# Second layer of a fused convolution kernel: the skip term by ACT, end terms on all rows, a narrower output projection, a new order

## The chip, the cores and the metric

One core of one Trainium2 chip. The time is device microseconds of one execution. The engines are named PE (matmul), DVE, ACT, POOL (elementwise) and SP (which issues the DMAs); each runs its instructions in its own program order and waits on semaphores for the others.

## What is computed

Two layers run one after the other on `x` of 8 x 128 x 128 x 128 (batch, channels, rows, columns), all in float32. The first, a dilated convolution with spectral attention, isn't touched. The second, cut to what matters:

```python
y = conv2d(x, conv_w, padding=1) + conv_b             # 128 -> 128 channels, 3 x 3
seq = y.reshape(B * H * W, 8, 16)                     # the channels of a position: 8 tokens of 16
xi, z = split(seq @ in_proj_w.T)                      # 32 + 32
xc = silu(conv1d(xi))                                 # 4 taps along the tokens
dt, Bm, Cm = split(xc @ x_proj_w.T)                   # 1 + 16 + 16
dt = softplus(dt * dt_proj_w + dt_proj_b)
h = exp(dt * A) * h + dt * Bm * xc                    # a state of 32 x 16, token after token
ym = (sum(h * Cm) + D * xc) * silu(z)
out = ym @ out_proj_w.T                               # back to 128 channels
return x + silu(group_norm(out))
```

## The kernel before

The second layer, `layer1`, works on 256 blocks of 4 image rows (512 positions, `N`). A block's channels are on the 128 partitions, as 4 tokens x 32 inner channels for half of the 8 tokens (`hf` 0 or 1). The state of a position has 32 x 16 entries for each token. It is spread over the partitions as 16 states x 8 channels, with the 32 channels in four groups of 8 (`NG`). A step `s` from 0 to 15 is one token `t = s // 2` and two of the four groups, so a tile has 128 x 2 x 512 elements. The steps that the prediction names:

- `spread_a s` (L824, PE) writes dt times A into a PSUM pair, `exps s` (L835, ACT) takes its exponential in place, `decay s` (L855; L853 for the last token) multiplies it by the state of the token before, in place, and `add s` (L860) adds the new input: both on DVE. The pair is free after add (for s of 14 and 15 after decay).
- `spread_u s` (L824, PE) writes the inputs dt * xc into a PSUM pair, and `inject s` (L847, DVE) multiplies them by B; the pair is free after inject. For s in 4, 5 and 10 POOL does it from a copy laid out by DMA (L845).
- `weigh s` (L866, POOL) multiplies the state by C, and `collect t` (L922, PE) sums the states into `yps`.
- Terms that need no recurrence are taken apart: at the first and the last token the product of a token's own B and C is summed over the states by `ends_sum` (L896, PE, from L888 on POOL), multiplied by the inputs in `own_terms` (L902, DVE), and added to `yps` by `own_add` (L906, PE). The skip term D * xc is written into `yps` by `skip` (L915, PE), which opens the sum of each half.
- `gated hf` (L929, DVE) reads `yps` and multiplies by silu(z); `project_out` (L937, PE), `result` (L947, ACT) and `keep` (L960, SP) end a block. The group norm of an image follows when its last block is out (`norm`), and then `last_load`, `last_act` (L1012), `last_sum` (L1018) and `last_store` finish one block's rows in each pass.

A spread has two matmuls of 32 rows each: for even `s` they use rows 0 to 63 of the array, for odd `s` rows 64 to 127.

PSUM is full: three pairs of banks (slots 0, 1 and 2, the last argument of a spread and of `project_x` and `project_z`), one bank `pm` for all else, and one for `yps`. So a spread waits for the release of what was in its slot before.

No scheduler is at work. The program order of every engine is the written-out list `ORDER`; one pass goes through the list, and each entry says which step it issues, for which block (relative to the pass), and with which arguments:

```python
for i in range(-4, nb + 3):
    for f, ahead, *k in ORDER:
        if live(i + ahead):
            f(i + ahead, *k)
```

So `(exps, 0, 9)` is step 9 of the pass's own block and `(conv, 3, 0)` the first tap of the convolution of the block three ahead. In the text "add 10" is the step with `s` of 10, "a13" and "u2" stand for spread_a 13 and spread_u 2, and a half is written behind the name (skip 0, gated 1).

Of the kernel before, what the change touches and what calls it, by code (L numbers as in the profile page):

```python
# [9 lines left out]
F32 = mybir.dt.float32  # L10
# [6 lines left out]
P = 128  # L17
# [22 lines left out]
def _fields(widths):  # L40
# [13 lines left out]
    ("half", NH * L), ("group", P), ("ends", 4 * NH * DI), ("place", P),  # L54
# [13 lines left out]
def _constants():  # L68
# [42 lines left out]
    put(c1, C1, "place", (k[:, None] == i[None, :] // LP) & (i % LP == np.where(i < DI, 0, LP - 1)[:, None]))  # L111
# [479 lines left out]
def layer1(ctx, tc, x1, w1, c1, out):  # L591
# [34 lines left out]
    place = cf("place")  # L626
# [6 lines left out]
    m_o = const.tile([P, NH, L, G], F32, name="m_o")  # L633
# [8 lines left out]
    with tc.tile_pool(name="l1_prep", bufs=2) as prep:  # L642
# [18 lines left out]
        for hf in range(NH):  # L661
            for l in range(L):
                k = hf * L + l
                nc.vector.tensor_scalar(m_o[:, hf, l, :], wf("out_w"), cf("half")[:, k:k + 1], None, ALU.mult)
# [27 lines left out]
    LAST = (2, 6)  # L692
# [185 lines left out]
    def lay_own(i):  # L878
        d = st8[i]
        d["us"] = wk1.tile([NH * DI, N], F32, name="us")  # L880
        for e, l in enumerate((0, LP - 1)):
            u = d["u", e].rearrange("(d l) n -> l d n", l=LP)
            nc.sync.dma_start(d["us"][e * DI:(e + 1) * DI, :], u[l])
# [6 lines left out]
    def ends_sum(i):  # L890

        d = st8[i]
        d["pm"] = misc()
        for q in range(4):
            for e in range(NH):
                nc.tensor.matmul(  # L896
                    d["pm"][e * DI:(e + 1) * DI, q, :], ends[:, q, e, :], d["cb"], start=True, stop=True)

    def own_terms(i):
        d = st8[i]  # L900
        d["own"] = wk2.tile([NH * DI, N], F32, name="own")
        nc.vector.tensor_mul(d["own"], flat(d["pm"])[0:NH * DI], d["us"])  # L902

    def own_add(i, e):
        d = st8[i]
        nc.tensor.matmul(  # L906
            d["yps"], place[e * DI:(e + 1) * DI, :], d["own"][e * DI:(e + 1) * DI, :], start=False, stop=False,
            skip_group_check=True)

    def skip(i, hf):  # L910
        d = st8[i]
        d["yps"] = p_y.tile([P, N], F32, name="yps")
        for g in range(NG):
            a = slice(g * DI, (g + 1) * DI)
            nc.tensor.matmul(  # L915
                d["yps"][a], m_d[:, a], d["xc"][:, hf, :], start=True, stop=False, skip_group_check=True)
# [14 lines left out]
    def project_out(i, k):  # L931
        d = st8[i]
        if k == 0:
            d["pm"] = misc()
        for n in range(k * RB, (k + 1) * RB):
            j, hf = n // NH, n % NH
            nc.tensor.matmul(  # L937
                d["pm"][:, j, :], d["ym", hf][:, j * C:(j + 1) * C], m_of[:, hf, :],
                start=(hf == 0), stop=(hf == NH - 1))
# [58 lines left out]
    loaded, active = [], []  # L998
# [16 lines left out]
    def last_sum(i):  # L1015
        if active:
            b, r, v, res = active[0]
            nc.gpsimd.tensor_add(res, res, v)  # L1018

    def last_store(i):  # L1020
        if active:
            b, r, v, res = active.pop(0)
            nc.sync.dma_start(out[b, :, r:r + RB, :], res)  # L1023
# [3 lines left out]
        (load, 4), (skip, -1, 1), (add, 0, 3), (keep, -2), (spread_u, 0, 8, 1), (exps, 0, 4), (inject, 0, 9),  # L1027
        (decay, 0, 4), (inject, 0, 8), (end_products, 0), (spread_a, 0, 5, 2), (inject, 0, 5), (turned, 2),
        (exps, 0, 5), (lay_own, 0), (add, 0, 4), (decay, 0, 5), (collect, -1, 4), (collect, -1, 7),
        (last_act, -1), (collect, -1, 5), (spread_a, 0, 6, 0), (spread_u, 0, 11, 1), (project_dt, 1, 0),  # L1030
        (lay_states, 0, 1, 1), (add, 0, 5), (spread_u, 0, 13, 2), (weigh, 0, 2), (inject, 0, 11), (exps, 0, 6),
        (spread_a, 0, 7, 1), (softplus, 1, 0), (last_sum, -1), (lay_inputs, 0, 5), (own_add, -1, 1),
        (decay, 0, 6), (collect, -1, 6), (ends_sum, 0), (inject, 0, 13), (add, 0, 6), (exps, 0, 7),
        (weigh, 0, 3), (weigh, 0, 4), (own_terms, 0), (spread_a, 0, 8, 0), (weigh, 0, 5), (gated, -1, 1),
        (exps, 0, 8), (spread_a, 0, 9, 2), (decay, 0, 7), (project_bc, 1, 0), (skip, 0, 0), (states, 1, 0),
        (decay, 0, 8), (weigh, 0, 6), (add, 0, 7), (collect, 0, 1), (add, 0, 8), (exps, 0, 9), (decay, 0, 9),
        (project_bc, 1, 1), (spread_of, -2), (states, 1, 1), (spread_u, 0, 12, 1), (weigh, 0, 7),
        (inputs, 1, 0), (lay_states, 1, 0, 0), (inject, 0, 10), (own_add, 0, 0), (spread_a, 0, 11, 0),
        (add, 0, 9), (inject, 0, 12), (store_inputs, 1, 2), (project_dt, 1, 1), (lay_inputs, 1, 2),
        (exps, 0, 11), (decay, 0, 11), (collect, 0, 3), (collect, 0, 2), (spread_a, 0, 10, 2),  # L1040
        (softplus, 1, 1), (spread_u, 1, 1, 1), (exps, 0, 10), (add, 0, 11), (project_out, -1, 0),
        (project_out, -1, 1), (inject, 1, 1), (spread_a, 0, 13, 0), (spread_u, 1, 2, 1), (weigh, 0, 9),
        (result, -1), (lay_ends, 1), (exps, 0, 13), (decay, 0, 10), (inputs, 1, 1), (conv, 3, 0), (add, 0, 10),
        (inject, 1, 2), (decay, 0, 13), (spread_a, 0, 12, 2), (exps, 0, 12), (add, 0, 13), (decay, 0, 12),
        (conv, 3, 1), (project_x, 2, 1), (silu_x, 2), (last_store, -1), (weigh, 0, 10), (project_z, 2, 0),
        (conv, 3, 2), (weigh, 0, 8), (add, 0, 12), (silu_z, 2), (spread_u, 1, 0, 1), (gated, 0, 0),
        (weigh, 0, 15), (weigh, 0, 14), (spread_a, 0, 15, 2), (inject, 1, 0), (conv, 3, 3),
        (spread_a, 1, 2, 1), (spread_u, 1, 3, 0), (lay_states, 1, 1, 0), (exps, 0, 15), (weigh, 0, 12),
        (lay_states, 1, 0, 1), (decay, 0, 15), (weigh, 0, 11), (conv, 3, 4), (inject, 1, 3),
        (store_inputs, 1, 5), (spread_u, 1, 7, 2), (spread_a, 0, 14, 0), (exps, 1, 2), (conv, 3, 5),  # L1050
        (decay, 1, 2), (conv, 3, 6), (last_load, 1), (inject, 1, 7), (spread_u, 1, 6, 2), (add, 1, 2),
        (weigh, 0, 13), (spread_a, 1, 3, 1), (exps, 0, 14), (conv, 3, 7), (exps, 1, 3), (decay, 0, 14),
        (inject, 1, 6), (decay, 1, 3), (conv, 3, 8), (inject, 1, 4), (spread_u, 1, 9, 2), (biased, 3),
        (spread_a, 1, 4, 0), (norm, -3), (turn, 3),
# [23 lines left out]
    with tc.manual_schedule(engines={E.PE, E.Activation, E.DVE, E.Pool, E.SP}):  # L1078
        for i in range(-4, nb + 3):
            for f, ahead, *k in ORDER:  # L1080
                if live(i + ahead):
                    f(i + ahead, *k)
        i = nb
        while tails or loaded or active:
            last_load(i)
            last_act(i)
            last_sum(i)
            last_store(i)
# [90 lines left out]
```

## Time and profile before

| | |
|---|---|
| time, median of 3 runs | 13987.08 us (13984.85 to 13987.69) |
| the profiled execution | 13980.7 us; span of the trace 13978.8 us |
| granted TensorE clock | 0.991 |
| PE, DVE, ACT, POOL busy | 97%, 88%, 65%, 89% of the span |
| layer 0 | up to about 2050 us |
| layer 1 | 256 blocks, xc (L748) first at 2049.8 us and last at 13777.6 us |

A line of a group in the profile names the source line, the engine, the operation, the tiles written and read with their shapes, and the count; then busy time, mean duration in ns, and the idle time ahead of it with what ended it. A row of a timeline has the start in us, the duration, the same names, and in brackets the idle time before it with its releaser. A matmul in float32 is two instructions in the trace, each with a weight load (PEld).

### The profile page before, as it was taken

To read this page: it belongs to the slowest core of one execution; us is meant where nothing else is said; L and a number is where in the kernel's file an instruction comes from. 1 tells how busy PE (TensorE), PEld (TensorE's weight loads), DVE (VectorE), ACT (ScalarE), POOL (GpSimd) and SP (SyncE) were. 2 spreads that over 40 slices of the span, in tenths; PEclk is the share of its full clock that TensorE was granted. 3 is DMA by queue.
4 is the path that set the end of the run, shared out by engine and by line. 5 is a ranking of instruction groups with operands and counts; after the bars stand their busy time and mean duration, and the time that the engine had idled before them with its cause. 6 is when DMAs were issued, how large, how long until landed. Compare 5 with 4: busy or idle time off the path is not lost. (4 is left out here: it accounts for less than half of the span.)

```text
span 13978.8 us, 215719 instructions
## 1 busy us (share of the span) xinstructions
PE 13516.8 (97%) x77864; PEld 5468.2 (39%) x77864; DVE 12280.7 (88%) x11971; ACT 9099.3 (65%) x10678; POOL 12431.6 (89%) x6788
## 2 busy tenths in 40 slices
PE   9999999999999999999999999999999999999996
PEld 5676673333333333333333333333333333333332
DVE  3343349999999999999999999999999999999997
ACT  3353356666677777777777777776777777777775
POOL 6656649999999999999999999999999999999996
PEclk9999999999999999999999999999999999999998
DMA  4444446666666666666666666666666666767666
GB/s 134 151 124 123 143 121 133 137 139 134 140 153 156 153 151 154 151 158 152 151 152 153 157 149 157 152 153 153 152 157 151 152 154 153 156 147 157 153 153 178
DMA packets 1199723, 2077.87 MB, mean 149 GB/s; under 512 B 141376, under 2 KB 337984, under 8 KB 1190464
## 3 DMA queue, kind: packets, MB, share of 16 engines
q1 hardware_dynamic: 1198080, 2061.54, 64.0%
q8 instruction: 616, 10.09, 0.3%
q14 instruction: 451, 3.69, 0.1%
q10 hardware_dynamic: 576, 2.55, 0.0%
HBM read 822.01 MB, written 234.88 MB: 76 GB/s over the span
## 5 line engine op out<-in xcount | busy, mean ns | idle before, releaser
L866 POOL TENSOR_TENSOR hc<-h,cc 128x1024 f32<-128x1024 f32 x3584 | 8377.5, 2371 | 655.7 <-PE yps L922 281.3
L835 ACT ACTIVATE s<-s 128x1024 f32<-128x1024 f32 x3584 | 3615.5, 1009 | 2956.7 <-PE s L824 2942.4
L824 PE MATMUL s<-dt,m_a 32*128 32x512 f32 x14336 | 3764.4, 641 | 255.8 <-DVE h L860 189.4
L860 DVE TENSOR_TENSOR h<-s,h 128x1024 f32<-128x1024 f32 x3072 | 3724.5, 1219 | 98.4 <-POOL hc L866 0.9
L855 DVE TENSOR_TENSOR s<-s,h 128x1024 f32<-128x1024 f32 x3072 | 3743.6, 1224 | 8.9 <-ACT s L835 6.6
L847 DVE TENSOR_TENSOR h<-s,bb 128x1024 f32<-128x1024 f32 x2816 | 3420.9, 1215 | 191.0 <-PE s L824 170.1
L824 PE MATMUL s<-u,l_ct 32*128 32x512 f32 x11264 | 3184.0, 641 | 9.0 <-DVE h L860 3.7
L135 PE MATMUL pm<-xin,l_wt 128*128 128x508 f32 (+1 forms) x4608 | 2436.5, 629 | 5.7 <-DVE wk L645 5.0
L845 POOL TENSOR_TENSOR h<-ud,bb 128x1024 f32<-128x1024 f32 x768 | 1825.7, 2377 | 13.3 <-DMA ud<-uw 9.5
L922 PE MATMUL yps<-hc,l_ct 128*32 128x512 f32 x14336 | 1747.4, 598 | 0.9 <-POOL hc L866 0.9
L824 PEld LDWEIGHTS s<-dt,m_a 32*128 32x128 f32 x14336 | 1001.4, 183 | 1470.7 <-DVE h L847 687.4
L824 PEld LDWEIGHTS s<-u,l_ct 32*128 32x128 f32 x11264 | 852.3, 183 | 1420.5 <-issue 809.1
L135 PEld LDWEIGHTS pm<-xin,l_wt 128*128 128x128 f32 x4608 | 729.8, 188 | 1603.4 <-issue 1408.8
L835 ACT ACT_TABLE_LOAD x992 | 1272.7, 1283 | 22.7 <-PE s L824 3.6
L922 PEld LDWEIGHTS yps<-hc,l_ct 128*32 128x32 f32 x14336 | 387.7, 109 | 1200.4 <-issue 984.2
L775 POOL TENSOR_TENSOR u<-dt,xc 128x512 f32<-128x512 f32 x512 | 653.3, 1276 | 50.4 <-ACT dt L770 50.4
L770 ACT ACT_TABLE_LOAD x511 | 655.6, 1283 | 28.7 <-PE pm L765 0.7
L853 DVE TENSOR_TENSOR hc<-s,hc 128x1024 f32<-128x1024 f32 x512 | 623.2, 1217 | 36.1 <-ACT s L835 9.8
L765 PE MATMUL pm<-xc,m_dt 128*128 128x512 f32 x1024 | 577.2, 646 | 1.4 <-ACT yT L737 0.7
L937 PEld LDWEIGHTS pm<-m_o,ym 128*128 128x128 f32 x4096 | 476.5, 191 | 194.8 <-ACT dt L770 192.7
L915 PE MATMUL yps<-xc,m_d 128*32 128x512 f32 x4096 | 548.0, 607 | 0.1
L906 PE MATMUL yps<-own,l_ct 32*128 32x512 f32 x1024 | 547.3, 614 | 0.0
(193 smaller groups left out, 14097.9 us busy)
## 6 DMA issues: line engine op xcount, KB each, us to landing
bb<-all_b SPq DMA_DIRECT2D x1792, 256.0 KB, 5.7
cc<-all_c SPq DMA_DIRECT2D x1792, 256.0 KB, 5.7
ud<-uw SPq DMA_DIRECT2D x1536, 256.0 KB, 4.5
xin<-x SPq DMA_DIRECT2D x152, 768.0 KB, 5.1
xin<-x SPq DMA_DIRECT2D x112, 640.0 KB, 7.1
gn<-xr SPq DMA_DIRECT2D x256, 256.0 KB, 4.2
v<-gn SPq DMA_DIRECT2D x224, 256.0 KB, 4.0
res<-x SPq DMA_DIRECT2D x224, 256.0 KB, 3.3
```

What stands on the lines that cost most here:

```text
L135: nc.tensor.matmul(out[:, a:b, wa:wb], wt[:, t, :], src[:, r + dy + a - base:r + dy + b - base, wa + dx:wb + dx], start=(n == 0), stop=(n ...
L770: nc.scalar.activation(d["dt", hf], flat(d["pm"]), AF.Softplus, bias=wf("dt_b"))
L775: nc.gpsimd.tensor_mul(d["u", hf], d["dt", hf], d["xc"][:, hf, :])
L824: nc.tensor.matmul(d[name, s][:, q], m[a:a + DI, t % LP, :], d[src, t // LP][a:a + DI, :], start=True, stop=True)
L835: nc.scalar.activation(da, da, AF.Exp)
L845: nc.gpsimd.tensor_mul(h, d["ud", t][:, k:k + GP, :], state_row(i, "bb", t))
L847: nc.vector.tensor_mul(h, d["ups", s], state_row(i, "bb", t))
L853: nc.vector.tensor_mul(d["hc", s], da, d["hc", s])
L855: nc.vector.tensor_mul(da, da, d["h", s - GP])
L860: nc.vector.tensor_add(h, d["da", s], h)
L866: nc.gpsimd.tensor_mul(hc, d["h", s if t < L - 1 else s - GP], state_row(i, "cc", t))
L922: nc.tensor.matmul(d["yps"][g * DI:(g + 1) * DI], gather[:, t % LP, :], d["hc", GP * t + g // GP][:, g % GP], start=False, stop=t in LAST, ...
```

## The change

Four things in `layer1`:

- `skip` is an ACT instruction that writes D * xc into `yps`, and the matmuls of the half add to it. Only the first half of block 0 is still opened by PE.
- The end terms are held in 128 rows of 256 columns, not 64 rows of 512: `lay_own` lays the inputs out with four DMAs, `ends_sum` writes four groups of 32 partitions, and `own_add` adds with eight matmuls of 128 rows, 32 outputs and 256 columns, not with one of 32 rows, 128 outputs and 512 columns.
- `project_out` gives each half its own 64 output columns (4 tokens x 16), where before both halves were added up in 128.
- `ORDER` is new. `last_sum` hands over to a list of its own, which `last_store` reads.

```diff
-    put(c1, C1, "place", (k[:, None] == i[None, :] // LP) & (i % LP == np.where(i < DI, 0, LP - 1)[:, None]))
+    put(c1, C1, "place", np.stack([
+        (i // DI == h)[:, None] & (k[:, None] == i[None, :] // LP) & (i % LP == (0, LP - 1)[h % NH])[None, :]
+        for h in range(2 * NH)], 1))
...
-    m_o = const.tile([P, NH, L, G], F32, name="m_o")
+    m_o = const.tile([P, NH, LP, G], F32, name="m_o")
...
-            for l in range(L):
-                k = hf * L + l
-                nc.vector.tensor_scalar(m_o[:, hf, l, :], wf("out_w"), cf("half")[:, k:k + 1], None, ALU.mult)
+            for l in range(LP):
+                nc.vector.tensor_scalar(m_o[:, hf, l, :], wf("out_w"), same4[:, l:l + 1], None, ALU.mult)
...
-    LAST = (2, 6)
+    LAST = (3, 6)
...
-        d["us"] = wk1.tile([NH * DI, N], F32, name="us")
+        d["us"] = wk1.tile([P, N // 2], F32, name="us")
         for e, l in enumerate((0, LP - 1)):
             u = d["u", e].rearrange("(d l) n -> l d n", l=LP)
-            nc.sync.dma_start(d["us"][e * DI:(e + 1) * DI, :], u[l])
+            for h in range(2):
+                a = (h * NH + e) * DI
+                nc.sync.dma_start(d["us"][a:a + DI, :], u[l][:, h * (N // 2):(h + 1) * (N // 2)])
...
         for q in range(4):
             for e in range(NH):
+                a = (q // 2 * NH + e) * DI
                 nc.tensor.matmul(
-                    d["pm"][e * DI:(e + 1) * DI, q, :], ends[:, q, e, :], d["cb"], start=True, stop=True)
+                    d["pm"][a:a + DI, q % 2, :], ends[:, q, e, :], d["cb"], start=True, stop=True)
...
-        d["own"] = wk2.tile([NH * DI, N], F32, name="own")
-        nc.vector.tensor_mul(d["own"], flat(d["pm"])[0:NH * DI], d["us"])
+        d["own"] = wk2.tile([P, N // 2], F32, name="own")
+        nc.vector.tensor_mul(d["own"], flat(d["pm"])[:, 0:N // 2], d["us"])
...
     def own_add(i, e):
         d = st8[i]
-        nc.tensor.matmul(
-            d["yps"], place[e * DI:(e + 1) * DI, :], d["own"][e * DI:(e + 1) * DI, :], start=False, stop=False,
-            skip_group_check=True)
+        for h in range(2):
+            for g in range(NG):
+                a = slice(g * DI, (g + 1) * DI)
+                nc.tensor.matmul(
+                    d["yps"][a, h * (N // 2):(h + 1) * (N // 2)], place[:, h * NH + e, a], d["own"],
+                    start=False, stop=False, skip_group_check=True)

     def skip(i, hf):
         d = st8[i]
         d["yps"] = p_y.tile([P, N], F32, name="yps")
-        for g in range(NG):
-            a = slice(g * DI, (g + 1) * DI)
-            nc.tensor.matmul(
-                d["yps"][a], m_d[:, a], d["xc"][:, hf, :], start=True, stop=False, skip_group_check=True)
+        if i == 0 and hf == 0:
+            nc.tensor.matmul(d["yps"], m_d, d["xc"][:, hf, :], start=True, stop=False, skip_group_check=True)
+        else:
+            nc.scalar.mul(d["yps"], d["xc"][:, hf, :], wf("D"))
...
             nc.tensor.matmul(
-                d["pm"][:, j, :], d["ym", hf][:, j * C:(j + 1) * C], m_of[:, hf, :],
-                start=(hf == 0), stop=(hf == NH - 1))
+                d["pm"][:, j, hf * (W // 2):(hf + 1) * (W // 2)], d["ym", hf][:, j * C:(j + 1) * C], m_of[:, hf, :],
+                start=True, stop=True)
...
-        for i in range(-4, nb + 3):
+        for i in range(-4, nb + 2):
```

The new list, in full:

```python
ORDER = (
    (load, 4), (lay_inputs, 0, 5), (spread_u, 0, 11, 1), (spread_a, 0, 6, 0), (decay, 0, 5),
    (softplus, 1, 0), (inject, 0, 11), (add, 0, 5), (exps, 0, 6), (weigh, 0, 3), (collect, -1, 5),
    (weigh, 0, 5), (ends_sum, 0), (own_terms, 0), (spread_a, 0, 7, 1), (weigh, 0, 4), (decay, 0, 6),
    (exps, 0, 7), (spread_a, 0, 8, 2), (decay, 0, 7), (project_bc, 1, 0), (add, 0, 6), (collect, -1, 6),
    (add, 0, 7), (own_add, -1, 1), (exps, 0, 8), (states, 1, 0), (gated, -1, 1), (project_bc, 1, 1),
    (states, 1, 1), (spread_u, 0, 13, 0), (decay, 0, 8), (inject, 0, 13), (skip, 0, 0), (add, 0, 8),
    (spread_a, 0, 9, 1), (exps, 0, 9), (project_dt, 1, 1), (inputs, 1, 0), (own_add, 0, 0),
    (collect, 0, 1), (decay, 0, 9), (softplus, 1, 1), (weigh, 0, 6), (spread_a, 0, 11, 0),
    (spread_u, 0, 12, 2), (weigh, 0, 7), (project_out, -1, 0), (project_out, -1, 1), (add, 0, 9),
    (lay_states, 1, 0, 0), (inject, 0, 12), (exps, 0, 11), (spread_u, 1, 1, 1), (spread_a, 0, 10, 2),
    (result, -1), (collect, 0, 2), (collect, 0, 3), (decay, 0, 11), (inputs, 1, 1), (conv, 3, 0),
    (inject, 0, 10), (inject, 1, 1), (lay_ends, 1), (exps, 0, 10), (weigh, 0, 9), (add, 0, 11),
    (decay, 0, 10), (weigh, 0, 8), (store_inputs, 1, 5), (spread_u, 1, 2, 1), (add, 0, 10), (inject, 1, 2),
    (spread_a, 0, 13, 0), (exps, 0, 13), (conv, 3, 1), (spread_a, 0, 12, 2), (decay, 0, 13), (add, 0, 13),
    (weigh, 0, 11), (exps, 0, 12), (last_load, 0), (project_x, 2, 1), (lay_states, 1, 1, 0), (silu_x, 2),
    (weigh, 0, 10), (conv, 3, 2), (decay, 0, 12), (project_z, 2, 0), (last_act, 0), (spread_u, 1, 0, 1),
    (silu_z, 2), (store_inputs, 1, 2), (add, 0, 12), (spread_a, 0, 15, 2), (spread_u, 1, 3, 0),
    (inject, 1, 0), (spread_a, 1, 2, 1), (conv, 3, 3), (last_store, -1), (exps, 0, 15), (conv, 3, 4),
    (weigh, 0, 15), (gated, 0, 0), (inject, 1, 3), (spread_a, 0, 14, 0), (decay, 0, 15), (exps, 1, 2),
    (decay, 1, 2), (spread_u, 1, 7, 2), (weigh, 0, 14), (exps, 0, 14), (conv, 3, 5), (add, 1, 2),
    (inject, 1, 7), (conv, 3, 6), (spread_u, 1, 6, 2), (decay, 0, 14), (spread_a, 1, 3, 1), (exps, 1, 3),
    (conv, 3, 7), (weigh, 0, 13), (inject, 1, 6), (decay, 1, 3), (skip, 0, 1), (conv, 3, 8),
    (spread_a, 1, 4, 0), (weigh, 0, 12), (lay_inputs, 1, 2), (biased, 3), (spread_u, 1, 9, 2),
    (lay_states, 1, 0, 1), (exps, 1, 4), (collect, 0, 4), (norm, -2), (turn, 3), (spread_of, -1),
    (add, 1, 3), (spread_u, 1, 8, 1), (turned, 3), (keep, -1), (inject, 1, 9), (spread_a, 1, 5, 2),
    (decay, 1, 4), (project_dt, 2, 0), (inject, 1, 8), (end_products, 1), (inject, 1, 4), (collect, 0, 7),
    (inject, 1, 5), (weigh, 1, 2), (last_sum, 0), (exps, 1, 5), (lay_own, 1), (lay_states, 1, 1, 1),
    (add, 1, 4),
)
```

More of the change, by code (lines that the diff above doesn't have):

```diff
@@ L53 @@
     ("ident", P), ("spread", LP * P), ("gather", LP * DI), ("taps", KC * L), ("same4", LP),
-    ("half", NH * L), ("group", P), ("ends", 4 * NH * DI), ("place", P),
+    ("half", NH * L), ("group", P), ("ends", 4 * NH * DI), ("place", 2 * NH * P),
 ])
@@ L625, in layer1 @@
     ends = cf("ends").rearrange("p (q e d) -> p q e d", e=NH, d=DI)
-    place = cf("place")
+    place = cf("place").rearrange("p (h c) -> p h c", c=P)
     m_u = cf("spread").rearrange("p (l c) -> p l c", c=P)
@@ L996, in norm @@
             norm_of(b)
-    loaded, active = [], []
+    loaded, active, summed = [], [], []
     def last_load(i):
@@ L1016, in last_sum @@
         if active:
-            b, r, v, res = active[0]
+            b, r, v, res = active.pop(0)
             nc.gpsimd.tensor_add(res, res, v)
+            summed.append((b, r, res))
     def last_store(i):
-        if active:
-            b, r, v, res = active.pop(0)
+        if summed:
+            b, r, res = summed.pop(0)
             nc.sync.dma_start(out[b, :, r:r + RB, :], res)
     ORDER = (
-        (load, 4), (skip, -1, 1), (add, 0, 3), (keep, -2), (spread_u, 0, 8, 1), (exps, 0, 4), (inject, 0, 9),
@@ L1028, in layer1 @@
[L1028 to L1052, printed above, removed]
@@ L1053, in layer1 @@
-        (inject, 1, 6), (decay, 1, 3), (conv, 3, 8), (inject, 1, 4), (spread_u, 1, 9, 2), (biased, 3),
-        (spread_a, 1, 4, 0), (norm, -3), (turn, 3),
+        (load, 4), (lay_inputs, 0, 5), (spread_u, 0, 11, 1), (spread_a, 0, 6, 0), (decay, 0, 5),
+        (softplus, 1, 0), (inject, 0, 11), (add, 0, 5), (exps, 0, 6), (weigh, 0, 3), (collect, -1, 5),
+        (weigh, 0, 5), (ends_sum, 0), (own_terms, 0), (spread_a, 0, 7, 1), (weigh, 0, 4), (decay, 0, 6),
+        (exps, 0, 7), (spread_a, 0, 8, 2), (decay, 0, 7), (project_bc, 1, 0), (add, 0, 6), (collect, -1, 6),
@@ L1083, in layer1 @@
         i = nb
-        while tails or loaded or active:
+        while tails or loaded or active or summed:
             last_load(i)
```

## The prediction

> **What bounds the kernel now.** I read the page's shares first, then stretches of 1500 us, then the timelines of single engines.
>
> ```profile
> PE 13516.8 (97%) x77864; PEld 5468.2 (39%) x77864; DVE 12280.7 (88%) x11971; ACT 9099.3 (65%) x10678; POOL 12431.6 (89%) x6788
> ...
> DVE  3343349999999999999999999999999999999997
> ```
>
> The first line has the shares, the second the busy tenths by slice. DVE's low first six slices are layer 0 (to about 2050 us), which the change doesn't touch. In a stretch of layer 1 alone:
>
> ```profile
> 4900.00:6400.00 1500.00, 1464.81 (x8438) 519.11 (x8434) 1460.98 (x1318) 1064.74 (x1179) 1422.89 (x684) 1.00 0.68 152
> ```
>
> PE, DVE and POOL (first, third and fifth figure after the length) are all busy 95 to 98% of the time; ACT 71%. Three queues are nearly full, so no engine's own saving counts by itself. A layer-1 block recurs every 45.85 us (L915's second group at 7022.56 and 7068.41; over all 256 blocks L748's first and last start give 45.99, with the group norms). What closes that period is seen in the timelines of DVE and then PE:
>
> ```profile
> 7048.22 1.23 DVE L860 TENSOR_TENSOR h<-s,h 128x1024 f32<-128x1024 f32 x1
> 7049.36 1.21 DVE L847 TENSOR_TENSOR h<-s,bb 128x1024 f32<-128x1024 f32 x1
> ...
> 7055.28 0.68 DVE L929 TENSOR_TENSOR ym<-yps,zs 128x512 f32<-128x512 f32 x1
> 7056.61 1.22 DVE L847 TENSOR_TENSOR h<-s,bb 128x1024 f32<-128x1024 f32 x1 [0.65 <-PE s L824]
> ```
>
> ```profile
> 7049.50 1.13 PE L824 MATMUL s<-dt,m_a 32*128 32x512 f32 x4 [0.29 <-DVE h L860]
> 7050.55 1.12 PE L135 MATMUL pm<-xin,l_wt 128*128 128x508 f32 x2
> 7051.51 1.88 PE L743 MATMUL s<-yT,m_x 128*128 128x512 f32 x4
> 7053.32 1.13 PE L755 MATMUL s<-yT,m_z 64*128 64x512 f32 x4
> 7054.38 1.12 PE L135 MATMUL pm<-xin,l_wt 128*128 128x512 f32 x2
> 7055.43 0.70 PE L824 MATMUL s<-u,l_ct 32*128 32x512 f32 x2
> ```
>
> PE waits for DVE's add 10 to release a PSUM pair, runs six groups (7.1 us to 7056.61), and DVE waits for the last of them (spread_u 0) in inject 0. So the loop is: DVE from inject 0 (7010.76) to the end of add 10 (7049.46), 38.7 us, and PE from there to inject 0, 7.15 us: 45.85, the whole period. DVE's 38.7 is 38.12 of pure queue (31 starts of 1.13, the last 1.24, two short ones of 0.60, five of 0.13 more where an add directly follows its decay) and 0.58 of small waits. Pure queue per block: DVE 37 x 1.13 + 3 x 0.60 + 7 x 0.13 = 44.5; POOL 17 x 2.32 (seven L866 in 16.26 us) + 2 x 1.24 + 0.42 + 7/8 x 1.24 = 43.5; PE, adding start to start without its waits, 43.7.
>
> **What the Trainium skill says.** "TensorE: Matmul & The Clock Gate", Part 3: matmuls on different 32-row groups run together. The trace agrees, and it matters for what the change takes away:
>
> ```profile
> 7030.82 0.70 PE L824 MATMUL s<-dt,m_a 32*128 32x512 f32 x2
> 7030.83 0.69 PE L906 MATMUL yps<-own,l_ct 32*128 32x512 f32 x1
> ```
>
> The own-term matmul (row group 1) starts 0.01 us after a spread in rows 64 to 127; both are over at 7031.89. Same page, LDWEIGHTS (loading the stationary operand): a load costs its columns / 1.2 ns, 107 for 128. L937's 16 loads fill 1.86 us, 116 each, so that group is load-bound. "PSUM — Partial Sum Buffer", The four PSUM rules: ACT writes leave the has_written bits, and a matmul that doesn't open a group adds where they are set. No run here shows it; it is why block 0's first skip stays on PE. "ScalarE: Activation LUTs", What ACT_TABLE_LOAD costs: 1283 ns; the trace has 1283.
>
> **The change part by part**, per block.
>
> *Skip on ACT.* PE loses 16 instructions: 0.86 to 1.0 us a half, -1.9. ACT gains two 128x512 scaled copies, not in this trace: between L947 (598 ns, no pointer) and L1012 (814, two pointers); I take L956's 0.72 (one), so +1.4. They stand behind gated (DVE) and ahead of the own and collect matmuls, so two waits are new. skip 0 waits in ACT's queue for gated 1, with exps 9, softplus 1 and exps 11 behind it: with the queues laid end to end it starts 8.95 us and ends 9.7 us after decay 5, spread_a 9 ends at 10.4, exps 9 at 11.5, and decay 9 comes at 12.3, so 0.8 us is spare. own_add 0 waits for skip 0 on PE, with collect 1 behind, but PE gets there at 11. Both cost nothing while DVE's queue covers them.
>
> *Table loads.* With last_act between the two silus, loads fall from 992 + 221 for exp and L1012 to 774 + 0: 439 x 1.283 = 563 us less ACT. ACT isn't the bound; nothing, covered by DVE's queue. If L1012's transfer were late it would now hold silu_z and all exps behind it; by the queues it is issued some 9 us ahead, and page part 6 has v landing in 4.0.
>
> *Own terms in 128 rows.* DVE's L902 goes from 512 to 256 columns: 673 to about 425 ns (L440, 260 columns), -0.25 us. PE: ends_sum's 16 instructions spread over four column groups, not two: 1.04 to between 0.5 and 1.0, I take 0.6. own_add had been nearly free; now each is 16 instructions on all rows, which nothing in row groups can accompany. By L922's rate (8 of 512 columns in 0.88) 0.9; by L937's 124 ns each 2.0. I take 0.9, +1.7 over the two. lay_own issues four DMAs for two, about 1.2 us more on SP, which waits for all_b 9 us a block (2319.8 us in 256).
>
> *Output projection of 64 columns.* Half the streaming, but the same 16 loads of 128 columns: 1.98 to 1.85, floor 1.0 if loads were to overlap.
>
> *The order.* Spreads in different row groups pair: before, 10 pairs and 5 single slots; after, 11 pairs and 3, so -1.05 on PE. PE's sum becomes 43.7 - 1.9 + 1.7 - 0.45 - 0.15 - 1.05 = 41.9. DVE has six adjacent decay-add pairs for seven: 44.5 - 0.25 - 0.13 = 44.1. POOL stays at 43.5. last_load starts one block earlier after each norm and runs to the last block, so two, not four, output slices are left for the serial drain, where they come every 5.7 us (13902.23, 13907.91): -11 us once. The other SP steps move within slack (SP issues some 31 us of 45): lay_states 1 waits for POOL's inject 10, lay_inputs 2 for its own store, each several us ahead of its reader.
>
> Now the loop. add 10 no longer leads to spread_u 0 over a slot. In the new order slot 2 goes inject 12, spread_a 10, and PE runs from there without a wait that I find: spread_a 10 with u1 1.07, two collects 1.86, conv 1.05, a13 with u2 1.08, conv 1.05, a12 1.05, project_x 1.81, conv 0.95, project_z 1.06, u0 1.08, and 0.10 to DVE: 12.16 us. DVE from inject 0 to the end of inject 12: 26 x 1.13 + 1.21 + 2 x 0.60 + 0.36 + 3 x 0.13 = 32.5. Sum 44.7, where before it is 38.12 + 7.15 = 45.3. Small waits: before 0.58, of which 0.2 stood at decay 15 and goes; the rest scaled to the shorter stretch 0.32. New: inject 6 stands two places after inject 7, whose slot its spread needs: 1.25 + 1.13 against 2.26, 0.15. Period 45.2, against 45.85: -0.68 us x 256 = -174, and -11: -185. The profiled execution took 13980.7 us (span 13978.8), 0.05% under the median 13987.1; from the median, 13800.
>
> **Rivals.**
>
> *A, the loop above*, chance 0.55: 13800, own range 13720 to 13890 (0.3 us a block either way, for the small waits).
>
> *B, DVE's queue alone.* If the PE stretch is shorter than I count and small waits go, the period is 44.1 plus 0.2 to 0.6: 1.55 to 1.15 less, 13580 to 13680. For it: DVE's sum. Against it: inject 0 stood behind PE 256 times (170.1 us), and the PE stretch is now longer. 0.20.
>
> *C, half of it.* The new order puts two or three waits of 0.2 us elsewhere (inject 3 and exps 15 are within 0.2 to 0.3 of DVE): 13890 to 13958. 0.10.
>
> *D, slower: own_add pays by instruction.* The other loop is add 4, spread_a 6, then all of PE to u0 (27.4: the 41.9 less 14.5 for the groups after u0), then DVE from inject 0 to add 4, 16.85: 44.25, with small waits 44.95. It holds both own_adds, ends_sum and project_out. Each us per own_add counts twice, so at 1.35 each it equals 45.85 and the gain is gone; at L937's 124 ns it is 47.1, +1.3 x 256: up to 14310. For it: 32 new instructions per block, each with a weight load. Against: 32-column loads are cheap (L783: eight in 0.16 us). 0.11.
>
> *E, nothing measurable*, A and D offsetting or the ACT write not taking PE's work away in effect: 0.04. The instruction order shows L915 gone but for one group, so that the change doesn't do what it says is unlikely.
>
> **The numbers.** This kernel's runs tell about 0.2% (28 us) from no change. Faster: A, B and C, 0.85; same 0.04; slower 0.11. The range holds A, B down to 13610, and C: 13610 to 13965; D and the rest of B are left out.
>
> **What would show it.** Right: L929 to inject 0 still has a wait for PE, and PE's start of spread_a 10 follows inject 12; own_add near 0.9 a group; ends_sum near 0.6; L937's group still 1.8; no idle time of DVE behind ACT. Wrong: DVE without a wait at inject 0 (B), own_add groups above 1.35 (D), exps or decay 9 waiting behind skip (C or worse), POOL with less than 1 us of idle time per block.

## The result, and the profile after

The changed kernel takes 13861.68 us (median; 13859.87 to 13864.33), beside 13987.0 on the same chip before: a ratio of 0.9911, interval 0.9894 to 0.9928. That is 125 us less, where 185 were forecast. The profiled execution took 13860.26 us, span 13858.5.

The page's busy line and DVE's slices, which answer to the first two lines shown of before:

```profile
PE 13496.6 (97%) x80938; PEld 5526.0 (40%) x80938; DVE 12211.5 (88%) x11963; ACT 8814.3 (64%) x10753; POOL 12421.6 (90%) x6788
...
DVE  3343349999999999999999999999999999999997
```

PE has 3074 matmuls more and is busy 20 us less; the picture is the old one. The same 1500 us of layer 1 (after the length: PE, PEld, DVE, ACT, POOL):

```profile
4900.00:6400.00 1500.00, 1475.19 (x8888) 530.71 (x8882) 1465.38 (x1330) 1020.60 (x1186) 1434.81 (x691) 1.00 0.69 155
```

By this count all three full queues are a little fuller. PE went from 1464.81 to 1475.19: its instructions were to get 1.8 us a block shorter, and yet it seems nearer to the bound than before. The timelines show why. DVE's rows, with the add 5 of two blocks (L861 at 7023.27 and 7068.59) and inject 0 (7049.27):

```profile
7023.27 1.22 DVE L861 TENSOR_TENSOR h<-s,h 128x1024 f32<-128x1024 f32 x1
...
7049.27 1.23 DVE L848 TENSOR_TENSOR h<-s,bb 128x1024 f32<-128x1024 f32 x1 [0.28 <-PE s L825]
...
7068.59 1.21 DVE L861 TENSOR_TENSOR h<-s,h 128x1024 f32<-128x1024 f32 x1
```

PE's rows of the same block, without those between 7033.03 and 7047.04, none of which has a wait:

```profile
7023.66 2.01 PE L825 MATMUL s<-dt,m_a 32*128 32x512 f32 x8
7025.60 1.06 PE L784 MATMUL pm<-xc,m_bc 128*32 128x512 f32 x8
7026.48 1.04 PE L931 MATMUL yps<-hc,l_ct 128*32 128x512 f32 x8
7027.34 1.05 PE L913 MATMUL yps<-own,l_ct 128*32 128x256 f32 x16
7028.20 1.04 PE L784 MATMUL pm<-xc,m_bc 128*32 128x512 f32 x8
7029.18 1.13 PE L825 MATMUL s<-u,l_ct 32*128 32x512 f32 x4
7030.14 1.02 PE L825 MATMUL s<-dt,m_a 32*128 32x512 f32 x4
7031.09 1.13 PE L766 MATMUL pm<-xc,m_dt 128*128 128x512 f32 x2
7032.15 1.07 PE L913 MATMUL yps<-own,l_ct 128*32 128x256 f32 x16
7033.03 1.04 PE L931 MATMUL yps<-hc,l_ct 128*32 128x512 f32 x8
...
7047.04 1.13 PE L756 MATMUL s<-yT,m_z 64*128 64x512 f32 x4
7048.10 1.13 PE L825 MATMUL s<-u,l_ct 32*128 32x512 f32 x4
```

The first row is a7 and a8 in one; it lasts 2.01 us because a8 stands in it until add 5 has ended at 7024.49 and left slot 2. From a8 (7024.53) PE runs without a pause to u0 (7048.10), and inject 0 waits for u0. So the loop is: PE from a8 to the start of inject 0, 24.74 us, DVE from there to the end of the next add 5 (7069.80), 20.53. Sum 45.27; the period is 45.31 (L825's u0 at 7002.79 and 7048.10), before 45.85. It is not the loop of the forecast, which runs over inject 12 and a10.

A busy PE is in part a waiting one. Two spreads that were to run side by side start one after the other where the second waits for its slot, and the first counts as busy meanwhile. Here are u0, a15, u3 and a2:

```profile
7002.79 1.13 PE L825 MATMUL s<-u,l_ct 32*128 32x512 f32 x4
7003.73 1.13 PE L825 MATMUL s<-dt,m_a 32*128 32x512 f32 x4
7004.69 1.02 PE L825 MATMUL s<-u,l_ct 32*128 32x512 f32 x4
7005.24 1.13 PE L825 MATMUL s<-dt,m_a 32*128 32x512 f32 x4
```

a15 begins when add 12 has ended on DVE (7003.67), a2 when inject 0 has (7005.19). The next group starts at 7006.30, so the four take 3.51 us, where two pairs take 2.1: 1.4 us of waiting. In the same block a5 costs 0.35 us in this way, a6 0.28 and a8 0.88, and PE stands idle for 0.50 ahead of u6. Without them the 45.31 us become 41.9, and that is the PE sum of the forecast. So PE's instructions did get shorter; the time went into waits, most of which the busy share does not show.

Of the pieces, in the same 1500 us (busy time and mean ns of one, then idle time ahead), two of before and then four of after:

```profile
L906 PE MATMUL yps<-own,l_ct 32*128 32x512 f32 x132 | 70.5, 613 | 0.0
L937 PE MATMUL pm<-m_o,ym 128*128 128x128 f32 x528 | 67.7, 281 | 0.0
...
L913 PE MATMUL yps<-own,l_ct 128*32 128x256 f32 x1056 | 69.9, 382 | 0.0
L946 PE MATMUL pm<-m_o,ym 128*128 128x64 f32 x528 | 66.0, 278 | 0.0
L924 ACT ACTIVATE yps<-xc,l_wt 128x512 f32<-128x512 f32 x66 | 45.5, 689 | 3.3
L906 DVE TENSOR_TENSOR own<-pm,us 128x256 f32<-128x256 f32 x33 | 13.7, 414 | 0.0
```

The own term matmuls on PE (L913) come to as much as the old L906 had (70.5 us), L946 to hardly less than L937 (67.7). By starts, an own_add takes 0.86 to 0.88 us (7027.34 to 7028.20, 7032.15 to 7033.03). The skip on ACT takes 689 ns, with 0.05 us of idle time ahead of it on average.

**Where the 120 us of span lie.** I take L749's starts (L748 before), one a block. 255 distances at 45.31 for 45.85 give -137.7; the first block starts 3.3 us sooner; from the last start to the end it is 191.0 for 201.2, so -10.2. The seven passes with a group norm go the other way: in before each is 7.0 us longer than a plain one (52.5 to 53.2), in after 11.6 (55.8 to 58.4), +32. These come to -119 of the 120. One such pass of after, on DVE and then on PE:

```profile
3627.11 3.94 DVE L982 TENSOR_SCALAR dm<-st,mv 128x32 f32<-128x32 f32 x1
3631.09 0.19 DVE L983 TENSOR_TENSOR dm<-dm 128x32 f32<-128x32 f32 x1
```

```profile
3632.06 0.35 PE L988 MATMUL pm<-mv,l_ct 128*128 128x2 f32 x2 [3.68 <-DVE mv L986]
...
3637.31 2.08 PE L825 MATMUL s<-dt,m_a 32*128 32x512 f32 x4
```

An instruction on 32 columns takes 3.94 us, and after 3.68 us of idling PE takes 2.08 us for a spread that takes 1.13 elsewhere. The third figure from the end of these rows is the granted clock of PE, in this pass of after and in the corresponding one of before:

```profile
3633.20:3643.30 10.10, 8.75 (x28) 2.90 (x28) 7.74 (x11) 5.80 (x9) 2.35 (x1) 0.50 0.40 122
...
3701.20:3707.90 6.70, 4.75 (x20) 2.62 (x24) 4.77 (x14) 3.00 (x4) 0.39 (x1) 0.50 0.67 170
```

PE runs at half the clock for 10.2 us here and for 6.8 in before; over the seven passes it is 10.2 to 13.7 us in after and 3.4 to 6.8 in before.

### The profile page after: what moved, and what is told of

Same layout as the page of the kernel before. It is cut to its first block, busy times and chain, and to the rows that moved or that the text cites. A ratio compares the mean times of both kernels' runs of the same rounds, so it can differ in the third digit from the quotient of the medians.

```text
span 13858.5 us, 222678 instructions
## 1 busy us (share of the span) xinstructions
PE 13496.6 (97%) x80938; PEld 5526.0 (40%) x80938; DVE 12211.5 (88%) x11963; ACT 8814.3 (64%) x10753; POOL 12421.6 (90%) x6788
## 5 line engine op out<-in xcount | busy, mean ns | idle before, releaser
L825 PE MATMUL s<-dt,m_a 32*128 32x512 f32 x14336 | 3968.2, 638 | 25.4 <-DVE h L861 13.6
L861 DVE TENSOR_TENSOR h<-s,h 128x1024 f32<-128x1024 f32 x3072 | 3725.8, 1220 | 71.4 <-DVE s L856 1.4
L825 PE MATMUL s<-u,l_ct 32*128 32x512 f32 x11264 | 3164.1, 638 | 143.8 <-DVE h L848 134.5
L137 PE MATMUL pm<-xin,l_wt 128*128 128x508 f32 (+1 forms) x4608 | 2341.4, 617 | 5.9 <-DVE wk L647 5.2
L931 PE MATMUL yps<-hc,l_ct 128*32 128x512 f32 x14336 | 1852.3, 602 | 2.7 <-ACT away L964 2.7
L846 POOL TENSOR_TENSOR h<-ud,bb 128x1024 f32<-128x1024 f32 x768 | 1808.2, 2371 | 10.2 <-DMA ud<-uw 10.2
L825 PEld LDWEIGHTS s<-dt,m_a 32*128 32x128 f32 x14336 | 1106.2, 184 | 1431.1 <-DVE h L861 531.8
L825 PEld LDWEIGHTS s<-u,l_ct 32*128 32x128 f32 x11264 | 868.7, 184 | 1371.3 <-DVE h L848 555.2
L137 PEld LDWEIGHTS pm<-xin,l_wt 128*128 128x128 f32 x4608 | 772.5, 189 | 1476.9 <-issue 1258.9
L946 PEld LDWEIGHTS pm<-m_o,ym 128*128 128x128 f32 x4096 | 476.6, 192 | 194.4 <-ACT dt L771 192.6
L913 PE MATMUL yps<-own,l_ct 128*32 128x256 f32 x8192 | 542.0, 382 | 0.1
L784 PE MATMUL pm<-xc,m_bc 128*32 128x512 f32 x4096 | 539.3, 598 | 2.3 <-ACT all_b L791 1.4
```

Source lines behind the costliest of these rows:

```text
L137: nc.tensor.matmul(out[:, a:b, wa:wb], wt[:, t, :], src[:, r + dy + a - base:r + dy + b - base, wa + dx:wb + dx], start=(n == 0), stop=(n ...
L825: nc.tensor.matmul(d[name, s][:, q], m[a:a + DI, t % LP, :], d[src, t // LP][a:a + DI, :], start=True, stop=True)
L846: nc.gpsimd.tensor_mul(h, d["ud", t][:, k:k + GP, :], state_row(i, "bb", t))
L861: nc.vector.tensor_add(h, d["da", s], h)
L931: nc.tensor.matmul(d["yps"][g * DI:(g + 1) * DI], gather[:, t % LP, :], d["hc", GP * t + g // GP][:, g % GP], start=False, stop=t in LAST, ...
```

## The experiments

Times are medians; ratios are to the kernel before on the same chip, with a 95% interval. The experiments ran in three groups (e1 to e4, e5 to e8, e9 to e11), and before took 13988.26, 13981.19 and 13984.26 beside them, so I compare ratios, and turn them into us with 13985.

### Each edit undone: the skip of half 0 (e1), of half 1 (e2), the projection (e3), all of the order (e4)

e1 and e2 put one half's skip back on PE, in the place that it has in the new list:

```diff
-        if i == 0 and hf == 0:
-            nc.tensor.matmul(d["yps"], m_d, d["xc"][:, hf, :], ...)
+        if hf == 0 or i == 0 and hf == 0:          # e2: hf == 1
+            for g in range(NG):
+                nc.tensor.matmul(d["yps"][a], m_d[:, a], d["xc"][:, hf, :], ...)
```

> The kernel after, with skip of half 0 put back on PE as four matmuls of 512 columns at its place in the list; half 1 stays on ACT. Theory 1 (the period is closed by one loop: add 5 on DVE frees the pair of spread_a 8, PE then runs without a pause up to spread_u 0, inject 0 waits for that, and DVE runs back to add 5): the 0.87 us lie inside PE's part of the loop, so the period rises from 45.31 to about 46.2 and the time by 0.87 x 256 = 220 us. Theory 2 (DVE's own queue sets the period, PE is beside it): within 30 us of the kernel after. Theory 3 (what counts is PE's sum, wherever its work lies): also plus 220 here, told apart by the next run.

> The kernel after, with skip of half 1 put back on PE; half 0 stays on ACT. In the list it stands after spread_a 3 and the conv taps, in the part of the block where PE waits 0.5 us for inject 7 and a third of a us each for inject 9 and add 4. Theory 1: outside PE's part of the loop, so most of it goes into those waits: 0 to 80 us slower. Theory 2: within 30 us. Theory 3 (PE's sum): plus 220 us, as in the run before.

Measured: e1 14163.71, ratio 1.0125 (1.0108 to 1.0142), so 0.0214 or 299 us above the changed kernel. e2 14118.28, 1.0093 (1.0078 to 1.0108), 255 us above. PE in e1:

```profile
7020.35 1.13 PE L825 MATMUL s<-u,l_ct 32*128 32x512 f32 x4
7021.41 1.07 PE L924 MATMUL yps<-xc,m_d 128*32 128x512 f32 x8
7022.40 1.13 PE L825 MATMUL s<-dt,m_a 32*128 32x512 f32 x4
7023.46 1.12 PE L766 MATMUL pm<-xc,m_dt 128*128 128x512 f32 x2
```

Start to start, the skip is 0.99 us, and the spreads on its two sides are 1.06 each, where they had 0.96 and 0.95. So a group of 32-column matmuls between two groups of 32-row matmuls costs 0.21 us more than its own length. That makes 1.20, and the period grew by 1.19 (46.50): every us put between a8 and u0 is in the period, as the loop says; PE's sum, the third theory, would say the same. e2's skip lies outside that stretch, on the part of PE that feeds DVE. Its group is 1.00, and conv 7 and conv 8 around it take 1.05 each, 3.10 for 1.91, so 1.19 more; the period grew by 1.11 (46.42). DVE waits in it where it had not:

```profile
7033.52 1.23 DVE L848 TENSOR_TENSOR h<-s,bb 128x1024 f32<-128x1024 f32 x1 [0.61 <-PE s L825]
```

This is inject 9. PE's lead there was no more than 0.6 us, so my first theory for e2, that work outside the loop is nearly free, is wrong, and of the three PE's sum fits best. The trace has another reading: from u6, which waits 0.50 us for inject 7, to inject 9 PE is one more link in a chain over both engines, with 0.6 us to spare and no place for 1.2. e7, below, tells the two apart.

e3 has the projection of 128 columns:

```diff
-                    d["pm"][:, j, hf * (W // 2):(hf + 1) * (W // 2)], ..., start=True, stop=True)
+                    d["pm"][:, j, :], ..., start=(hf == 0), stop=(hf == NH - 1))
```

> The kernel after, with the output projection of before: 128 output columns for each half, summed in PSUM. The group of 16 instructions took 1.98 us before and 1.93 after. Weight loads as the limit: 1.98 again, inside the loop, so plus 0.05 x 256 = 13 us, within 30 us of the kernel after. Streaming as the limit: plus 0.5 to 1 us a block, 130 to 250 us.

Measured: 13876.57, ratio 0.992 (0.9905 to 0.9935), 13 us above the changed kernel by the ratios, 15 by the medians. That is within the interval, but the traces agree, with a period of 45.37 for 45.31: half the columns streamed, and 0.05 us a block won. The group's time does not go with the columns. That the loads of the stationary operand fill it in either form, as the prediction has it from 116 ns a load, fits this.

e4 has all the edits, and the list of before:

```diff
-        (load, 4), (lay_inputs, 0, 5), (spread_u, 0, 11, 1), (spread_a, 0, 6, 0), (decay, 0, 5),
+        (load, 4), (skip, -1, 1), (add, 0, 3), (keep, -2), (spread_u, 0, 8, 1), (exps, 0, 4), (inject, 0, 9),
...
```

> All the code of the change (skip on ACT, end terms in 128 rows, 64 columns) under the old list, which still has the last Silu between two exps, the group norm a pass later and one more pass at the end. Theory 1: the old loop (DVE from inject 0 to add 10, then PE from spread_a 12 to spread_u 0) holds none of the matmuls that changed; only own_terms on DVE is in it, 0.25 us shorter: a period of 45.6, so 13987 - 64 = 13920 us. If the edits carry the gain and the order nothing: 13862, as the kernel after. If the order alone carries it: 13987, or slower where the own matmuls, no longer beside a spread, get in the way (plus 0.8 us a block each that isn't hidden).

Measured: 14198.08, ratio 1.015 (1.0135 to 1.0165), 210 us slower than before, where the first theory had 13920. The edits alone lose. PE's longest wait, by what was waited for (us in total, times, longest us):

```profile
PE yps L931 <- ACT yps L924: 200.7, 254, 0.8
```

Collect 1 waits for the skip on ACT. I took this for the cause; e10, below, has the same wait at the same size, and it costs next to nothing.

### The old end terms in the new order (e6), and everything old in the new order (e8)

```diff
-                nc.tensor.matmul(
-                    d["yps"][a, h * (N // 2):(h + 1) * (N // 2)], place[:, h * NH + e, a], d["own"], ...)
+        nc.tensor.matmul(
+            d["yps"], place[e * DI:(e + 1) * DI, :], d["own"][e * DI:(e + 1) * DI, :], ...)
```

lay_own, ends_sum and own_terms likewise. e8 has this, both skips on PE, and the projection of 128 columns.

> The changed kernel with the old end terms alone: 64 rows of 512, ends_sum in two column groups, own_add one matmul of 32 rows. Theory 1 (a matmul of 32 rows is free only right beside a spread of the other 64 rows, and the new order puts both own_adds beside collects): each own_add takes 0.9 to 1.0 us as against 0.87, ends_sum 1.04 as against 0.57, so the loop from add 5 to spread_u 0 grows by 0.1 to 0.4 us, and the kernel by 25 to 100 us, to 13885 to 13960. Rival (the old own_add stays nearly free, so that the new form is a price that the change paid): 2 x 0.87 us less on PE, half of it at least off the loop, 13440 to 13640.

> The new order with all the old code: skip by PE in both halves, end terms in 64 rows, projection of 128 columns. The three edits undone one at a time cost 302 (skip of half 0), 257 (skip of half 1) and 15 us. Theory 1 (the order is made for the edits and is worth nothing without them; the two skips lie on the same loop): 13862 + 302 + 257 + 15 and 25 to 100 for the end terms, 14450 to 14540; somewhat less if the skips hide in one wait, down to 14350. Rival (the order brings most of the gain, whatever the code): 13860 to 13987.

Measured: e6 13995.61, ratio 1.0011 (1.0004 to 1.0018), 140 us above the changed kernel, more than the 25 to 100 expected. PE in e6:

```profile
7038.23 1.04 PE L923 MATMUL yps<-hc,l_ct 128*32 128x512 f32 x8
7039.20 1.12 PE L905 MATMUL yps<-own,l_ct 32*128 32x512 f32 x2
7040.26 1.07 PE L782 MATMUL pm<-xc,m_bc 128*32 128x512 f32 x8
```

One matmul takes 1.06 us (7039.20 to 7040.26), and the collect ahead of it 0.97, not 0.86. From that collect to a11 e6 has 8.04 us where the changed kernel has 7.53; the period is 45.82, 0.51 more. So in this order the new form isn't a price that the change paid: among 32-column groups it is 0.2 us shorter than the single matmul, and spares the switch. The 0.40 us that ends_sum gained does not count: e6 has its a7 and a8 in 1.61 us, the changed kernel in 2.01, the difference being a8's wait for add 5.

e8 took 14566.45, ratio 1.0419 (1.0402 to 1.0436), 710 us above the changed kernel. The four edits undone one by one are 299 + 255 + 13 + 140 = 707. They add up, as work in one chain does; PE's sum would add up too.

### One own_add left out (e7)

```diff
-        (own_add, 0, 0), (collect, 0, 1),
+        (collect, 0, 1),
```

> The changed kernel without own_add of half 0: the first token's own terms are left out of the output. PE has 0.87 us a block less, inside the loop from add 5 to spread_u 0. Theory 1 (several loops stand within 0.2 us of each other: inject 12 to spread_a 10, inject 2, inject 7): the next loop takes over at once, so the gain is 0 to 60 us, 13800 to 13862. Rival (PE's sum closes the period): 0.87 x 256 = 223 us, 13640.

Measured: 13785.39, ratio 0.986 (0.9846 to 0.9875), 71 us below the changed kernel, a little past the expected 60, and a third of the 223 that PE's sum would give: PE is not the bound by its sum, however e1, e2 and e8 look. 0.87 us less between a8 and u0 makes the period 45.00, 0.31 less. What closes now is seen in u1 and a10, which ran side by side, and don't:

```profile
7047.94 1.13 PE L825 MATMUL s<-u,l_ct 32*128 32x512 f32 x4
7048.48 1.13 PE L825 MATMUL s<-dt,m_a 32*128 32x512 f32 x4
```

a10 (second row) begins 0.06 us after inject 12 ends on DVE (7047.21 + 1.21). From one a10 (7003.49) to the next it is 44.99: this is the loop of the forecast, which stood 0.3 us behind the other.

### One edit alone in the kernel before: the skip (e10), the end terms (e11)

```diff
-            nc.tensor.matmul(
-                d["yps"][a], m_d[:, a], d["xc"][:, hf, :], start=True, stop=False, skip_group_check=True)
+            nc.scalar.mul(d["yps"], d["xc"][:, hf, :], wf("D"))
```

e11 has, in place of this, lay_own, ends_sum, own_terms and own_add of the change.

> The kernel before, with its own order, and only the skip term on ACT. Theory 1 (in the old order ACT reaches the skip too late: it waits there for gated with exps behind it, and collect 1 waits for ACT, 0.8 us a block in the run with all edits): slower by 100 to 210 us, 14090 to 14190, with a wait of PE for ACT's write of yps. Rival (the loop is the one of the prediction, which holds no skip; taking 1.9 us off PE neither helps nor hurts): 13960 to 14010. A third way (PE's sum counts here as it does in the new order): faster by 100 to 400.

> The kernel before, with its own order, and only the end terms in 128 rows. Theory 1 (in the old order the own matmuls run beside a spread nearly free, and the new ones cannot: 2 x 0.87 us more on PE, less 0.45 of ends_sum; PE feeds DVE's part of the loop with 0.3 to 0.6 us to spare): slower by 100 to 300 us, 14090 to 14290. Rival (DVE's stretch from inject 0 to add 10 covers it, and DVE's own term gets 0.25 us shorter there): faster by up to 64 us, 13920 to 13990. With the run of the skip alone the two should add to about the 211 us of all edits in the old order if the costs are separate.

Measured: e10 13998.06, ratio 1.001 (1.0001 to 1.0018), 14 us slower; e11 14144.02, 1.0114 (1.0097 to 1.0131), 159 us slower. Together 173 of e4's 210. PE's waits by releaser in e10, and in e11:

```profile
PE yps L924 <- ACT yps L917: 200.1, 254, 0.8
```

```profile
PE s L826 <- DVE h L862: 18.3, 16, 4.2
```

In the old order the skip on ACT leaves 0.79 us of waiting on PE in the place of the skip itself; the rival was right, the loop of before holds no skip, and the period is the old one (45.9). Its 14 us are the norm passes, each 2 us longer. The end terms are the cost: in e11 PE waits for an add 18.3 us in all, where before did 193.1, and is busy 1486.86 of the 1500 us. So the loop of before no longer closes the block, which now takes 46.49; that PE's own stretch does is likely, not shown, since its busy time holds waits. The old own matmul ran beside a spread there nearly for nothing; the new one, on all rows, does not.

### The group norm: in pieces (e5), and on ACT (e9)

e5 spreads its steps over the list without changing one:

```diff
-        (collect, 0, 4), (norm, -2), (turn, 3),
+        (norm_m2, -2), (collect, 0, 4), (turn, 3),
...
-        (add, 0, 8),
+        (add, 0, 8), (norm_a, -2),
...
-        (collect, 0, 2), (collect, 0, 3),
+        (collect, 0, 2), (norm_m1, -2), (collect, 0, 3),
```

> Only the order of the group norm's own steps differs from the changed kernel: its DVE, PE and ACT pieces stand at seven places of a pass, each a few us behind what it reads, not in one chain. Theory 1 (the seven passes with a norm cost 11.7 us more than a plain one because DVE, PE and ACT wait for each other step by step, and because ACT's table reload and PE's idle time follow): each falls to about 3 us, its pure work; 7 x 8.7 = 61 us less than the changed kernel's 13861.7, so about 13800, between 13785 and 13815. Rival (what the norm costs is its own work on DVE, and the slow stretch of PE after it comes whatever the order): within 10 us of 13862.

Measured: 13853.13, ratio 0.9909 (0.9894 to 0.9924), 3 us below the changed kernel, which the interval doesn't tell from none: the rival, or rather its result. The norms now lengthen two passes each, by 78 us in all, where 81 had been. DVE, and PE behind it:

```profile
6520.41 1.58 DVE L1026 TENSOR_SCALAR dm<-st,mv 128x32 f32<-128x32 f32 x1
...
6522.25 1.14 DVE L1028 SCALAR_TENSOR_TENSOR dm<-dm,st 128x32 f32<-128x32 f32 x1
```

```profile
6526.35 2.08 PE L825 MATMUL s<-u,l_ct 32*128 32x512 f32 x4 [2.53 <-DVE h L861]
```

The small instructions still take over 1 us, and PE, after 2.53 us of idling, the doubled time. So the length is in DVE's instructions, not in their chain. e9 takes them off DVE, all but a reciprocal; the old form stays for the last image (two of its steps, cut):

```diff
-        nc.vector.tensor_scalar(dm, st[:, 0], 1.0 / N, mv[:, 0:1], ALU.mult, ALU.subtract)
-        nc.vector.tensor_mul(dm, dm, dm)
...
+        act(dm, st[:, 0], AF.Identity, scale=1.0 / HW, accum_out=q["mv"][:, 0:1])
+        act(dm, st[:, 0], AF.Square, bias=q["neg"], scale=1.0 / N, accum_out=q["s1"])
...
```

> The changed kernel with the group norm's small steps on ACT at places where ACT sits idle, but for one reciprocal on DVE; two matmuls on PE as before. Theory 1 (a norm pass costs 11.7 us because DVE's steps with two SBUF operands stand still until POOL's instruction ends, 1.2 to 5.2 us each, and PE then runs at half speed for some us): with nothing of it left on DVE each of the seven passes costs 0 to 3 us, so 7 x 8.7 to 7 x 11.7 = 61 to 82 us less than the changed kernel, near 13785, and the DVE row of those passes shows no instruction of 128 x 32 at all. Rival (the cost is the two small matmuls and the table load of the square root, which are still there): less than 20 us gained, 13840 to 13860.

Measured: 13786.89, ratio 0.9858 (0.9844 to 0.9873), 74 us below the changed kernel: the first theory, and a version faster than both kernels. No pass is longer than 46.3 us after the first blocks, though the small matmuls and the table load of the rival are still there. The same step on ACT:

```profile
3596.47 0.32 ACT L1027 ACTIVATE dm<-st,nneg 128x32 f32<-128x32 f32 x1
```

This and the seven rows around it, the norm's sums and squares, take 1.5 us (3595.66 to 3597.20), while ACT would have idled. What holds DVE is seen in the pass of after shown above. POOL, in that stretch:

```profile
3624.02 4.69 POOL L846 TENSOR_TENSOR h<-ud,bb 128x1024 f32<-128x1024 f32 x2
3628.65 2.36 POOL L867 TENSOR_TENSOR hc<-h,cc 128x1024 f32<-128x1024 f32 x1
```

POOL ends at 3631.01, L982 at 3631.05. In before the corresponding stall is L975, which ends at 3701.64 where POOL's L845 ends at 3701.59:

```profile
3699.38 2.26 DVE L975 SCALAR_TENSOR_TENSOR dm<-dm,st 128x32 f32<-128x32 f32 x1
...
3699.22 2.37 POOL L845 TENSOR_TENSOR h<-ud,bb 128x1024 f32<-128x1024 f32 x1
```

The same holds for all seven passes of both kernels: 37 of the norm's DVE instructions take more than 0.3 us, and each ends 0.04 to 0.05 us after an instruction of POOL. The eighth norm, after the last block, has POOL idle and no such instruction. The Trainium skill has this in "SBUF — State Buffer", Who interferes with whom: DVE and GpSimd share a pair of ports, held for a whole instruction, and DVE needs it for two inputs in SBUF or in a two-port mode. The ends agree with that to 0.05 us; no run moved POOL's instructions, so the port is argued, and what is shown is that the norm off DVE brings the time back. DVE's large instructions of the loop take one operand from PSUM and keep their 1.22 us beside POOL.

## Why the prediction was right or wrong

**Right:** the sign, the range, and the frame, a loop over PE and DVE. PE's sum is right too: 41.9, once the waits are taken out of the trace. Of the other terms: skip on ACT 0.689 us (0.72), own_terms 0.414 (0.425), ends_sum 0.57 by starts (0.6), own_add 0.86 to 0.88 (0.9, so rival D's price of 1.35 is far), table loads 774, the drain -10.2 us (-11), inject 6's wait 0.19 (0.15). DVE does wait at inject 0, has hardly any idle time behind ACT, and a10 follows inject 12 by 0.14 us.

**Too small a gain, first: which loop closes.** The step "Now the loop" took the successor of the old one, over slot 2 and a10, and called it the period. Another was just as long. For a8 and add 5 PE's stretch as the trace has it, 24.74, and DVE's at the forecast's prices, 20.15, make 44.89, more than loop A's 44.7; the prediction worked out only a neighbour of it, from add 4 and a6, and that for a rival. The trace has 45.27 for the a8 loop, and e7 has 44.99 for loop A once the other is shortened. So loop A's 45.2 was high by 0.2: the prediction had 0.47 of small waits in it, part of them scaled from before, and e7 leaves 0.29. The loop that it did not work out brought the period to 45.31: -0.54 for -0.68, some 36 us. That the forecast was no further off is in part luck, two errors of 0.2 and 0.3 us pulling opposite ways.

**Second: a cost that the prediction did not have.** The norm was moved with the rest, and its seven passes got 4.6 us longer each. They were left out of the sum, as if they stayed the same. The prediction asked of the moved DMA issues whether they had slack, and never asked beside which of POOL's instructions the norm would stand. In before its three instructions over 32 columns took 3.2 us together in every pass; in the new place they take 3.7 to 5.6, and PE, kept idle longer, runs at half the clock for 10.2 to 13.7 us, not 3.4 to 6.8. That is 32 us of the miss; e9 takes back 74 of the 81 us that the norms cost.

**Third: the skip's worth.** It was sized at -1.9 us on PE. By e1 and e2 it is 1.0 to 1.2 a half, since the switches on its two sides go with it: in the new order the skip is worth 554 us of 707. own_add was booked as +1.7 us, less 0.45 for ends_sum; against the old order e11 shows a loss of 0.64 us a block, while in the new one the old form would cost 140 us more. Those sums were made against before, step by step, with the order as an extra. The runs have neither half of the change paying alone:

| ratio to before | order of before | new order |
|---|---|---|
| code of before | 1 | 1.0419 |
| new code | 1.015 | 0.9911 |

The new list puts the own matmuls among 32-column groups and pairs the spreads with one another. By my reading it needs a PE without skips, and the new code needs a list in which the own matmuls had no free place anyway.

**Rivals.** B did not come: the period stayed 1.2 above DVE's own 44.1. C came close in size (13890 to 13958 against 13862) and in kind, near-ties elsewhere, but on PE's stretch from a8. E's reason, that ACT's write doesn't take PE's work away in effect, is true in the old order (e10).

## What to carry to other kernels

When three engines are nearly full, list every buffer's loop (release, engine, release) with the same prices and take the longest; the successor of the loop that closed before is only one of them, and here two stood within 0.3 us of each other. Price a matmul group together with its neighbours: the same own terms were free beside a spread, 0.87 us in one form among 32-column groups and 1.06 in another. And look at the rare passes by themselves: seven of 256 gave back a fifth of what the others gained, and moving fourteen small instructions a norm to an idle engine brought 74 us. Last, a busy share of 98% need not mean a full queue: in the block shown 2.9 us were waits of one spread beside another that was still running.

## What the runs showed of the hardware

- A group of 32-column matmuls put between two groups of 32-row ones lengthened each neighbour by 0.10 to 0.11 us (e1), and put between two convolutions on all rows by 0.19 for both together (e2).
- A DVE instruction of 128 x 32 with its operands in SBUF took 0.24 to 5.16 us (L982, eight times), by where POOL's instructions stood; L980 (a reduction) and L981 (one column) stayed at 0.18 and 0.15.
- PE's granted clock fell to 0.50, with spreads of 2.08 us for 1.13, around an idle time of 3.68 us in after and of 2.53 in e5. "TensorE: Matmul & The Clock Gate", Part 1, of the Trainium skill has the clock halved after an idle window of about 3.4 us that runs freely; in e5 it fell 1.8 us after PE's last work, so a shorter idle time was enough, and it came back after 9.5 us of work without a break (6526.35 to 6535.86). The half clock lasted 3.4, 6.8, 10.2 or 13.7 us in the seven passes of before and after, whole multiples of 3.41. In e9 it stayed at 1.00 from 3580 to 13600 us. In the 40 slices of the page none of this appears: PEclk is 9 throughout layer 1 but for the last.
